# Two 128-partition loads per chunk, weight sums on VectorE, M on two queues, and an early half of chunk 0 in a cross-network kernel

## The chip, the cores and the metric

The kernel runs on one core of one Trainium2 chip. The metric is the device time in microseconds (us) of one execution, as a median of several; lower is better. The profile gives the span from the first to the last instruction of one execution.

## The reference

```python
def _cin_forward(x, Ws, bs, fc_w, fc_b):          # x: (1024, 64, 16) float32
    x0 = h = x; xs = []
    for i in range(3):
        z = einsum('bfe,bge->bfge', x0, h)         # all products of features
        y = einsum('oc,bce->boe', Ws[i], z.reshape(B, -1, 16)) + bs[i]   # 128 channels
        if i != 2: x_i, h = y[:, :64], y[:, 64:]   # one half is output, one goes on
        else:      x_i = h = y
        xs.append(x_i)
    return sum(concat(xs, 1), axis=2) @ fc_w.T + fc_b      # (1024, 1)
```

Only one weighted sum of the last channels is wanted. So the channel sums of the weights, V0, V1 and V2 (64x64 each), can be formed first, and V2 folded into the second layer's weights as a tensor M. For each column (one sample, one of 16 positions) the kernel then needs h1, the upper half of layer one, and q, a quadratic form made with M plus V1 x; the result is the sum of (h1 + b) q + x (V0 x + c).

## The kernel before

1024 samples are cut into 32 chunks of 512 columns. For a chunk VectorE makes four tiles z of products of features (128 partitions x 2048), TensorE contracts them with 16 weight tiles, and a 17th tile zl (squares and x itself) closes the sum. The 128 output rows are h1 (64) and q (64). This is the loop:

```python
def products(c, j):
    z = zp.tile([128, NI, N], F32, tag="z", name="z")              # zp has bufs=3
    nc.vector.tensor_tensor(z, xas[c], xbs[c][:, j, :]...to_broadcast(...), ALU.mult)
    for i in range(NI):
        t = j * NI + i
        nc.tensor.matmul(accs[c], w_all[:, t, :], z[:, i, :], start=(t == 0), stop=False)
...
for c in range(NCH + 1):
    if c + 1 < NCH: load_chunk(c + 1)      # four 64-partition loads, and zl, xx
    if c < NCH: products(c, 0); products(c, 1)
    if c > 0:   combine(c - 1)             # q, uu; each second chunk y = V0 x and the sums
    if c < NCH: products(c, 2); products(c, 3); squares(c)
```

Ahead of it stands a setup, in which each step needs the one before:

```python
for k in range(32):                        # V2 on TensorE, a moving operand of one column
    nc.tensor.matmul(pv2[:, k:k+1], w2s[:, k, :], fc2, start=True, stop=True)
... v2t ...                                # M = V2 times layer two's upper weights
nc.tensor.matmul(pm, v2t[to], w1s[to, m*512:(m+1)*512], start=True, stop=True)
...
nc.scalar.dma_start(out=md[0:64, 0:64, :], in_=m_sb)       # M to DRAM, 5 writes
nc.scalar.dma_start(out=ms1[to]..., in_=skewed(...))       # and back, 11 skewed reads
... w_all[:, 0:NT, 64:128] = ms1 + ms2                     # the q half of the weights
# V0 and V1: 8 products with a two-column weight tile, rows spread by more transfers
```

## Time and profile before

| | before |
|---|---|
| median time | 554.61 us (552.36 to 554.63) |
| span of the profile | 555.0 us |
| chunk 0 starts on TensorE | 66.3 us |
| chunk 1 starts | 80.9 us |
| last contraction ends | 546.3 us |

Three kinds of lines are read below. A line of the chain that ended last has a start, a length and what the chain was in. A group of instructions has its busy time and the mean ns of one, then after the bar the idle time of the engine just before it and what ended that. A line of the windows has the stretch, its length, the busy time of TensorE, weight loads, VectorE, ScalarE and GpSimd (each with its number of instructions), the granted clock, the share of the 16 DMA engines, and GB/s.

PE is TensorE, PEld its weight loads, DVE VectorE, ACT ScalarE; L191 is line 191 of that run's kernel file. A row of 40 digits has the busy share (or, as PEclk, the granted clock) of each fortieth of the span, in tenths. A queue is the order in which one engine (SyncE or ScalarE) issues its transfers. A group of TensorE counts two instructions for each product in the code. The lines of the kernel before stand in the prediction.

### The profile page before, as it was taken

The page shows a single profiled execution, that of the slowest core. Times are in us where ns is not written, and L with a number is a line of the kernel's source. Part 1 is how long each engine was busy: PE and PEld are TensorE (multiplying, and loading weights), DVE is VectorE, ACT ScalarE, POOL GpSimd, SP SyncE. Part 2 cuts the span into 40 slices and gives each one's busy share as a digit, 9 for nine tenths or more (in the row PEclk, how much of TensorE's full clock was granted, in tenths as well). Part 3 has the DMA queues.
Part 4 walks back from the last instruction along what each step waited for, and adds up shares of the span by engine and source line. Part 5 has one row for each costly group of instructions (what it writes and reads, how often), then busy time and mean ns, then how long its engine had stood idle before and what let it go on. Part 6 is the DMA issues. An engine that isn't in the chain of part 4 may idle for free.

```text
span 555.0 us, 3402 instructions
## 1 busy us (share of the span) xinstructions
PE 515.9 (93%) x1240; PEld 231.9 (42%) x1240; DVE 352.0 (63%) x205; ACT 44.9 (8%) x81; POOL 5.3 (1%) x18
## 2 busy tenths in 40 slices
PE   5803799999999999999999999999999999999997
PEld 5600144444444444444444444444444444444442
DVE  0250076768677677768676867767776867686751
ACT  0100300000000000000000000000000000000001
POOL 3000000000000000000000000000000000000000
PEclk9967699999999999999999999999999999999999
DMA  8999998787777777877778777777787877874000
GB/s 254 185 283 210 205 208 170 144 163 146 156 153 159 150 152 162 180 161 161 160 147 165 146 154 154 154 150 154 161 180 161 165 155 151 162 152 77 0 1 0
DMA packets 33114, 85.33 MB, mean 154 GB/s; under 512 B 6405, under 2 KB 6949, under 8 KB 28710
## 3 DMA queue, kind: packets, MB, share of 16 engines
q1 hardware_dynamic: 29234, 81.84, 71.1%
q10 hardware_dynamic: 3608, 3.28, 2.8%
q8 instruction: 10, 0.16, 0.2%
q14 instruction: 6, 0.05, 0.0%
q0 software_dynamic: 256, 0.00, 0.0%
HBM read 82.89 MB, written 2.17 MB: 153 GB/s over the span
## 4 chain that ended last, share of the span: by engine, by line
PE 92%; DMA 6%; DVE 0%; ACT 0%; issue 0%; ACTq 0%; SPq 0%
PE acc L236 79%; PE acc L240 5%; DMA w<-in_wv 3%; PE pv L133 2%; PE y L254 2%; PE pv L197 2%; DMA ms<-md 1%; DMA fc<-in_fc_w 1%; DMA md<-m_sb 1%; PE pm L146 1%; PE po L281 0%; DVE acc L256 0%; DVE uu L255 0%; ACT res L289 0%; ACT q L249 0%
## 5 line engine op out<-in xcount | busy, mean ns | idle before, releaser
L236 PE MATMUL acc<-z,w_all 128*128 128x512 f32 x1024 | 447.2, 592 | 0.0
L231 DVE TENSOR_TENSOR z<-xa,xb 128x2048 f32<-128x2048 f32 x128 | 293.3, 2292 | 135.9 <-PE acc L236 134.6
L236 PEld LDWEIGHTS acc<-z,w_all 128*128 128x128 f32 x1024 | 194.5, 190 | 244.5 <-issue 244.4
L249 ACT COPY q<-acc 64x512 f32<-64x512 f32 x32 | 18.6, 582 | 443.8 <-PE acc L240 443.8
L197 PE MATMUL pv<-w,fc 128*2 128x512 f32 x16 | 11.5, 887 | 27.9 <-DMA w<-in_wv 14.9
L240 PE MATMUL acc<-zl,w_all 128*128 128x512 f32 x64 | 32.7, 592 | 0.0
L250 DVE SCALAR_TENSOR_TENSOR uu<-acc,bh,q 64x512 f32<-64x512 f32 x32 | 23.7, 740 | 10.0 <-ACT q L249 9.5
L239 ACT ACTIVATE zl<-xa 64x512 f32<-64x512 f32 x32 | 20.1, 628 | 3.6 <-DMA xa<-in_x 3.6
L133 PE MATMUL pv<-fc,w2s 128*128 128x1 f32 x64 | 13.8, 352 | 6.6 <-DMA fc<-in_fc_w 6.6
L256 DVE TENSOR_REDUCE acc<-uu 128x64 f32<-128x1024 f32 x16 | 19.5, 1220 | 0.5
L240 PEld LDWEIGHTS acc<-zl,w_all 128*128 128x128 f32 x64 | 12.2, 190 | 15.3 <-issue 15.3
L197 PEld LDWEIGHTS pv<-w,fc 128*2 128x2 f32 x16 | 1.6, 108 | 37.6 <-issue 21.5
L133 PEld LDWEIGHTS pv<-fc,w2s 128*128 128x128 f32 x64 | 13.7, 332 | 6.6 <-DMA fc<-in_fc_w 6.6
L254 PE MATMUL y<-xx,bd 128*128 128x512 f32 x32 | 16.3, 592 | 0.0
L136 DVE COPY v2t<-pv 64x32 f32<-64x32 f32 x2 | 0.4, 184 | 20.4 <-PE pv L133 20.4
L255 DVE SCALAR_TENSOR_TENSOR uu<-y,cx,xx 128x512 f32<-128x512 f32 x16 | 11.9, 745 | 0.0
L188 DVE TENSOR_TENSOR w_all<-ms,ms 128x1024 f32<-128x1024 f32 x1 | 1.2, 1224 | 13.2 <-DMA ms<-md 13.2
L254 PEld LDWEIGHTS y<-xx,bd 128*128 128x128 f32 x32 | 6.1, 190 | 7.7 <-issue 7.7
L199 ACT COPY vrow<-pv 2x512 f32<-2x512 f32 x8 | 4.2, 570 | 33.3 <-DMA ms<-md 32.2
L184 DVE MEMSET ms<- 64x64 f32 x1 | 0.1, 112 | 9.7 <-DMA ms<-md 9.7
L146 PE MATMUL pm<-w1s,v2t 64*64 64x512 f32 x16 | 5.6, 809 | 0.5 <-DVE v2t L137 0.5
L152 DVE COPY m_sb<-pm 64x512 f32<-64x512 f32 x4 | 2.7, 683 | 3.2 <-PE pm L146 3.2
(33 smaller groups left out, 21.0 us busy)
## 6 DMA issues: line engine op xcount, KB each, us to landing
xa<-in_x SPq DMA_DIRECT2D x64, 512.0 KB, 5.8
xb<-in_x SPq DMA_DIRECT2D x64, 512.0 KB, 7.1
zl<-in_x SPq DMA_DIRECT2D x32, 128.0 KB, 4.2
xx<-in_x SPq DMA_DIRECT2D x32, 128.0 KB, 4.1
w2s<-in_wv SPq DMA_DIRECT2D x4, 512.0 KB, 7.8
w<-in_wv SPq DMA_DIRECT2D x4, 512.0 KB, 11.9
w1s<-in_w1h SPq DMA_DIRECT2D x1, 1024.0 KB, 13.4
md<-m_sb ACTq DMA_DIRECT2D x2, 512.0 KB, 7.1
```

Of the source, the lines that this page charges most:

```text
L133: nc.tensor.matmul(pv2[:, k : k + 1], w2s[:, k, :], fc2, start=True, stop=True)
L146: nc.tensor.matmul(pm, v2t[to], w1s[to, m * 512 : (m + 1) * 512], start=True, stop=True)
L197: nc.tensor.matmul(pv, fc01, w01[:, m * 512 : (m + 1) * 512], start=True, stop=True)
L231: nc.vector.tensor_tensor(z, xas[c], xbs[c][:, j, :].unsqueeze(1).to_broadcast([128, NI, N]), ALU.mult)
L236: nc.tensor.matmul(accs[c], w_all[:, t, :], z[:, i, :], start=(t == 0), stop=False)
L239: nc.scalar.activation(zls[c][0:64], xas[c][0:64, 0, :], AF.Square)
L240: nc.tensor.matmul(accs[c], w_all[:, NT, :], zls[c], start=False, stop=True)
L249: nc.scalar.copy(q, accs[c][64:128])
L250: nc.vector.scalar_tensor_tensor(uu[to, 0, :], accs[c][0:64], bh1, q, ALU.add, ALU.mult)
L254: nc.tensor.matmul(y, bd, xxs[c // 2], start=True, stop=True)
L255: nc.vector.scalar_tensor_tensor(uu[:, 1, :], y, cx, xxs[c // 2], ALU.add, ALU.mult)
L256: nc.vector.tensor_reduce(acc[:, :, c // 2, :], uu.rearrange("p k (b e) -> p k b e", e=E), AX.X, ALU.add)
```

## The change

Its intent is to shorten the setup and to keep VectorE well ahead of TensorE. Each chunk comes in two 128-partition loads. V2, V1 and V0 are made by a multiply and a reduction on VectorE. M is written and read on two queues, and the reads stand ahead of the V1 weights and of chunk 1. The h1 half of chunk 0 is contracted while M is under way: 64 output rows leave room for two column halves of the array, each taking 256 of the chunk's columns. The program order is fixed by hand, with three products ahead of the evictions; V0 is made inside chunk 2.

```diff
+    ctx.enter_context(tc.manual_schedule())
-    zp = ctx.enter_context(tc.tile_pool(name="zp", bufs=3))
+    zp = ctx.enter_context(tc.tile_pool(name="zp", bufs=7))
...
     def load_chunk(c):
-        for half in range(2):                      # 64 partitions each
-            nc.sync.dma_start(out=xa[to], in_=rows(c, 0, [[1, NI]]))
-            nc.sync.dma_start(out=xb[to], in_=rows(c, 16 * half + 4, [[4, NJ]]))
-        ... zl and xx loaded too
+        nc.sync.dma_start(out=xa, in_=...)         # 128 partitions, 8 KB rows
+        nc.sync.dma_start(out=xb, in_=xrb[c])      # zl and xx copied by ScalarE
...
+    def weigh(w, fc, out):
+        nc.vector.tensor_tensor(w, w, fc...to_broadcast(...), ALU.mult)
+        nc.vector.tensor_reduce(out, w, AX.X, ALU.add)
-    for k in range(32):
-        nc.tensor.matmul(pv2[:, k : k + 1], w2s[:, k, :], fc2, start=True, stop=True)
+    for k in range(4):
+        weigh(w2s[k // 2][:, cols], fcr[:, 128:256], v2h[:, 8 * k : 8 * k + 8])
...
+    nc.scalar.dma_start(out=md[0:64, 0:32, :], in_=m_lo)
+    nc.sync.dma_start(out=md[0:64, 32:64, :], in_=m_hi)
+    ... three more on sync, two more on scalar
...
+    def side_by_side(p, part, tiles):
+        for t in tiles:
+            for n in range(2):
+                nc.tensor.matmul(p[halves[n]], w_all[:, t, cols],
+                    z[:, n * H2 : (n + 1) * H2], start=(t == 0), stop=(t == NT))
+    side_by_side(ph, 0, range(NT + 1))             # h1 of chunk 0, before M is back
+    ... M read on two queues, then w1x and chunk 1 loaded
+    side_by_side(pq, 1, range(NT))                 # q of chunk 0
...
-    for c in range(NCH + 1):
+    for c in range(1, NCH + 1):
+        if c > 2 and c % 2 == 0: v0x(c // 2 - 1)   # y, ahead of the products
+            for j in range(NJ - 1): products(c, j)
+        ... factors(c - 1)                         # q, uu
+        if c == 2: ... weigh(w0x, ...); v0x(0)     # V0 made here, y after 3 products
+        if c % 2 == 0: sums(c // 2 - 1)
+            products(c, NJ - 1); last_tile(c); contract_last(c)
```

## The prediction

> **What bounds the kernel now.** I read four views. First the page: TensorE is the busiest engine, but the slices show two phases.
>
> ```profile
> span 555.0 us, 3402 instructions
> PE   5803799999999999999999999999999999999997
> PEclk9967699999999999999999999999999999999999
> L236 PE MATMUL acc<-z,w_all 128*128 128x512 f32 x1024 | 447.2, 592 | 0.0
> L231 DVE TENSOR_TENSOR z<-xa,xb 128x2048 f32<-128x2048 f32 x128 | 293.3, 2292 | 135.9 <-PE acc L236 134.6
> ```
>
> The first five slices (about 66 us) have holes and a lower granted clock; after them TensorE is at 9 to the end. L236 never idles (last column 0.0), and VectorE's L231 waits 134.6 us for TensorE: in the main loop TensorE is the bound and VectorE has slack. Second, the chain that ended last, start and length:
>
> ```profile
> 0.76 5.75 DMA fc<-in_fc_w
> 6.55 13.83 PE pv L133 x64
> ...
> 24.52 4.45 DMA md<-m_sb
> ...
> 29.36 11.91 DMA w<-in_wv
> 41.41 3.50 PE pv L197 x4
> 44.92 6.70 DMA w<-in_wv
> ...
> 52.26 6.73 DMA ms<-md
> ...
> 59.61 6.33 PE pv L197 x8
> ...
> 66.32 13.93 PE acc L236 x32
> 80.25 0.86 PE acc L240 x2
> 81.11 13.73 PE acc L236 x32
> ```
>
> The loop begins at 66.3; before it lies a serial setup: V2 on TensorE, M, M to DRAM and back (ms), V0 and V1 on TensorE. Third, the windows view (stretch, length, busy of PE, PEld, DVE, ACT, POOL, clock, DMA share, GB/s):
>
> ```profile
> 6.00:12.00 6.00, 5.45 (x26) 5.45 (x26) 0.00 (x0) 0.00 (x0) 0.33 (x3) 1.00 1.08 397
> 14.00:26.00 12.00, 11.52 (x46) 8.58 (x46) 2.59 (x7) 2.12 (x4) 0.00 (x0) 1.00 1.03 200
> 38.60:63.00 24.40, 8.59 (x13) 1.25 (x14) 1.45 (x3) 3.10 (x6) 0.00 (x0) 0.64 1.03 219
> 66.30:546.30 480.00, 480.00 (x1120) 212.62 (x1120) 336.38 (x186) 35.22 (x65) 0.00 (x0) 1.00 0.72 146
> ```
>
> The queues are full at 397 GB/s while 128-partition weights load and at 200 while the 64-partition halves of chunk 0 load. The loop is 480 us of unbroken TensorE. Fourth, the timeline of the end: the last contraction ends at 546.3, the span 8.7 us later (q, uu, reduction, po, store).
>
> **The Trainium skill.** "DMA: Bandwidth & Descriptors", Rules for kernel authors, advises one 128-partition transfer in place of two to disjoint halves; the 397 against 200 GB/s agree. "VectorE: DVE Perf Modes", the perf-mode tier table, has fp32 tensor_tensor and tensor_reduce at one element per cycle, 2293 ns for 2048; the trace has 2292 for L231 and 1220 for a reduction of 1024. "TensorE: Matmul & The Clock Gate", Part 1, says that idle of a few us halves the clock for the next 3.4 us or so; the trace grants 0.64 in the gappy stretch. "TensorEngine Tiling (Array Packing)", Tiling Modes, lets two 128x64 column tiles work independently; no run here shows column tiles. The row halves of L146 do overlap: 16 instructions took 5.6 us including 0.8 us for evictions and a cold start.
>
> **Part by part.** (1) *Main loop.* A logical 512-column product is two instructions, 0.858 us (16 in 13.73). A chunk is 17 of them, 14.59 us; 31 chunks and 15 V0 products are 452.4 + 12.9 = 465.3 us, unchanged, since TensorE is already unbroken. Fixed order, seven z buffers and three products of lead therefore buy nothing in the steady loop. The larger x transfers (2 MB instead of 2.25 MB a chunk) are hidden at a DMA share of 0.72 as well. The new ScalarE copies (three of about 0.6 us a chunk) sit on an engine with 2 us of work per 14.6.
>
> (2) *V2 on VectorE.* Removed: 13.8 us of TensorE. Added: four pairs of multiply and reduce over 1024, 4 x (1.22 + 1.22) = 9.8 us, beginning when the first weights and the broadcast row land, about 6.7 (the old row landed at 6.5). With four 0.2 us copies v2t is ready at 17.4 instead of 20.8. The M products then start cold: two pieces at 1.7 us, two at 0.86, plus an eviction of 0.7: M is in SBUF at 23.6, where the last old eviction ended at 27.2.
>
> (3) *M through DRAM.* Old: writes issued from 24.5, reads from 38.6 to 63.0, 24.4 us, on one queue, sharing the transfers with V weights and chunk loads. New: two queues, and the reads stand ahead of the V1 weights and chunk 1. Write: 2.1 MB, 1.6 us to start, between 5 us (397 GB/s) and 10 us (200), 2 us to land: I take 34. Reads: five issues of 0.63 us per queue and some 6 us of transfer, then queueing: SyncE's waits show an issue waiting for an older, unrelated load (8.3 us for zl behind xa), so I expect the third read on ScalarE's queue to wait for a first one. I take 44.7 for the last landing, and w_all's second half at 46 (1.22 us), against 64.2.
>
> (4) *Chunk 0 split.* h1 (17 tiles) runs on TensorE in the shadow of (3), z of chunk 0 ending at about 34 on VectorE. After 46 only the other half of the columns remains: 34 products of 256 columns. If column halves overlap, 7.3 us (half of 14.6) up to 9 if weight loads show; plus 1.7 us because the clock has fallen during the wait: start of chunk 1 at about 55.5. If they do not overlap, 14.6 + 1.7: 62.5. V1 (2.29 + 2.29 + 0.4 on VectorE) ends at about 51, beside this, if its 1 MB has landed by 46.
>
> (5) *V0 and order.* In chunk 2 the fixed order puts y after the third product on TensorE, and on VectorE uu, the reduction and the fourth z after y. When TensorE has finished y, VectorE needs 0.75 + 1.22 + 2.29 + 0.2 = 4.5 us more: one stall of 4.5 us, perhaps 0.9 of cold clock after it. From chunk 4 on y stands ahead of the chunk's products; after the eviction of chunk c-1, VectorE needs 0.7 + 0.75 + 2 + 2.29 = 5.8 us for the fourth z, wanted at 11.2. No stall.
>
> Sum: start of chunk 1 + 465.3 + 5.4 + 8.7. With 55.5: 534.9. With 62.5: 541.9. In the old kernel the same sum is 66.3 + 14.6 + 465.3 + 8.7 = 554.9, against 555.0 seen. So the gain is about 25 us of chunk 0 and setup less 5 us given back in chunk 2.
>
> **Rivals.** *A: column halves run one after the other.* For: no column tiles in this trace. Against: the row halves overlap. Weight 0.35; 542. *B: M's way through DRAM stays long.* The old reads took 8 to 10 us to land beside other transfers, and V1 weights and two chunks follow right behind on SyncE's queue; then w_all comes at 50 to 52 and the total is about 540 (547 with A). *C: M quick and overlapped, no clock loss:* writes at 397 GB/s and 3 us less in reads give w_all at 41, total 528 to 530. *D: the loop stops being unbroken*, VectorE or ScalarE becoming the bound through the fixed order: VectorE's work is 336 us of 480, so only a wrong order in every chunk would do it; 0.04, and then 560 or more is possible. *E: the gain lies in the loop* (the lead removing VectorE's waits): L236's idle of 0.0 speaks against it; those 134.6 us are waits of the engine with slack.
>
> **Range.** Mixing 0.65 x 535 and 0.35 x 542 with a few us of M's path either way gives a centre near 536; C pulls down. I say 535, 527 to 544. Faster by over 2% means below 543.5: only A with B, or D, miss it: 0.87. Within 2%: 0.11. Slower: 0.02.
>
> **What would show it.** Chain: the loop starts (first chunk-1 product) at 52 to 63; L133 and L197 gone. Windows: TensorE unbroken after it but for one gap of 4 to 5 us some 26 us later, waiting for z. V2 reduction ends at 17, last M read lands at 42 to 48. The second pass over chunk 0 lasts 9 to 11 us if halves overlap, 15 to 17 if not. Spacing of full products stays 0.429 us per instruction, the tail 8.7. I am wrong if TensorE shows regular gaps in every chunk, if chunk 1 starts after 65, or if the chunk-2 stall is absent (then 5 us better).

## The result, and the profile after

| | before | after |
|---|---|---|
| median time | 554.62 us (4 runs) | 538.23 us (537.95 to 539.22, 4 runs) |
| span of the profile | 555.0 | 536.1 |
| chunk 1 starts | 80.9 | 55.9 |

The ratio is 0.9717, with a 95% interval of 0.969 to 0.9745: the mean time of the changed kernel's runs over that of the other's runs of the same rounds, so not quite the ratio of the medians. Executions over 1.5% slower than the fastest of the same kernel are left out of the means. The change is 2.8% faster.

The page of the changed kernel has these lines for those shown of before:

```profile
span 536.1 us, 3189 instructions
PE   0465996999999999999999999999999999999997
PEclk9987998999999999999999999999999999999999
L191 PE MATMUL acc<-z,w_all 128*128 128x512 f32 x992 | 432.8, 594 | 4.7 <-DVE z L182 4.7
L182 DVE TENSOR_TENSOR z<-xa,xb 128x2048 f32<-128x2048 f32 x128 | 284.5, 2281 | 1.6 <-DMA xb<-in_xrb 1.5
L214 DVE SCALAR_TENSOR_TENSOR uu<-acc,bh,q 64x512 f32<-64x512 f32 x31 | 23.1, 744 | 138.0 <-ACT q L213 138.0
L153 PE MATMUL pm<-w1s,v2t 64*64 64x512 f32 x16 | 5.9, 863 | 17.3 <-DVE v2t L143 17.3
L239 PE MATMUL pq<-z,w_all 128*64 128x256 f32 x64 | 8.4, 429 | 9.1 <-DVE w_all L280 9.1
```

The setup now takes four slices of 13.4 us instead of five of 13.9. VectorE's products no longer wait for TensorE (134.6 us before, nothing now); but VectorE's slack has only moved, for its uu now waits 138.0 us for q, the copy of a finished sum. TensorE, which never waited inside the loop before, now waits 4.7 us for a z (0.4 before chunk 1, 4.3 in chunk 2). The chain that ended last tells the setup and where those 4.7 us lie:

```profile
0.75 6.40 DMA fcr<-in_fc_w
...
17.26 5.93 PE pm L153 x16
...
25.17 8.63 DMA md<-m_sb
...
33.86 2.33 DMA md<-m_sb
...
37.81 4.62 DMA ms<-md
...
42.85 10.59 DMA xb<-in_xrb
...
53.56 2.30 DVE z L182
55.91 14.00 PE acc L191 x32
...
81.07 0.87 PE y L222 x2
...
81.96 0.76 DVE uu L226
...
83.89 2.29 DVE z L182
...
86.22 5.40 PE acc L191 x8
```

V2 is done at 17.2, M is written until 36.2 and its two large tiles are read until 44.6, and chunk 1 starts at 55.9. The chain reaches chunk 1 through its load (xb lands at 53.4) and its first z, which ends at 55.9; the second pass over chunk 0 had ended at 55.5. In chunk 2, y ends at 81.9, then uu, the reduction and the fourth z follow one another on VectorE, and TensorE resumes at 86.2. Eight instructions then take 5.40 us instead of 3.43. Four windows, of the second pass over chunk 0, the stall, the time after it, and the loop:

```profile
46.10:55.50 9.40, 9.38 (x76) 5.55 (x76) 6.87 (x5) 0.41 (x2) 0.00 (x0) 0.86 1.02 426
82.00:86.00 4.00, 0.00 (x0) 0.00 (x0) 3.97 (x3) 0.00 (x0) 0.00 (x0) 1.00 0.01 2
86.00:90.00 4.00, 3.78 (x5) 1.65 (x6) 4.00 (x3) 0.00 (x0) 0.00 (x0) 0.57 0.71 262
100.00:527.00 427.00, 427.00 (x996) 189.05 (x995) 291.01 (x167) 65.69 (x112) 0.00 (x0) 1.00 0.32 126
```

The granted clock is 0.57 in the 4 us after the stall, which is where the 2 us went. In the loop TensorE is again busy for every one of 427 us; the share of the DMA engines is 0.32, less than half of the 0.72 before.

The balance: chunk 1 starts 25.0 us earlier, chunk 2 gives back 4.3 us of stall and 2.0 of clock, and 25.0 less 6.3 is 18.7, against 18.9 in the spans. By stages of the two traces, the 25.0 are:

| stage | before | after | gain |
|---|---|---|---|
| M's last eviction ends | 27.2 | 23.9 | 3.3 |
| from there to w_all's second half | 37.0 | 22.1 | 14.9 |
| from there to chunk 0 (the second pass) | 2.0 | 0.1 | 1.9 |
| from there to chunk 1 | 14.7 | 9.8 | 4.9 |

The largest share is M's way through DRAM. The third line is the last of V0 and V1 on TensorE, which in the kernel before ended 2 us after the weights were ready.

### The profile page after: what moved, and what is told of

Read it like the earlier page. It is cut to its first block, busy times and chain, and to the rows that moved or that the text cites. A ratio compares the mean times of both kernels' runs of the same rounds, so it can differ in the third digit from the quotient of the medians.

```text
span 536.1 us, 3189 instructions
## 1 busy us (share of the span) xinstructions
PE 496.6 (93%) x1262; PEld 222.0 (41%) x1262; DVE 362.1 (68%) x222; ACT 79.1 (15%) x135; POOL 5.7 (1%) x18
## 3 DMA queue, kind: packets, MB, share of 16 engines
q1 hardware_dynamic: 12058, 74.82, 36.2%
## 4 chain that ended last, share of the span: by engine, by line
PE 89%; DMA 6%; DVE 3%; issue 0%; ACTq 0%; SPq 0%; ACT 0%; DVEq 0%
PE acc L191 80%; PE acc L205 5%; PE y L222 2%; DMA md<-m_sb 2%; DMA xb<-in_xrb 2%; DMA fcr<-in_fc_w 1%; PE pm L153 1%; DVE v2h L133 1%; DVE w L132 1%; DMA ms<-md 1%; DVE z L182 1%; PE po L354 0%; DVE uu L226 0%; DVE acc L227 0%; ACTq L271 0%
## 5 line engine op out<-in xcount | busy, mean ns | idle before, releaser
L191 PE MATMUL acc<-z,w_all 128*128 128x512 f32 x992 | 432.8, 594 | 4.7 <-DVE z L182 4.7
L191 PEld LDWEIGHTS acc<-z,w_all 128*128 128x128 f32 x992 | 188.9, 191 | 243.4 <-issue 230.0
L182 DVE TENSOR_TENSOR z<-xa,xb 128x2048 f32<-128x2048 f32 x128 | 284.5, 2281 | 1.6 <-DMA xb<-in_xrb 1.5
L214 DVE SCALAR_TENSOR_TENSOR uu<-acc,bh,q 64x512 f32<-64x512 f32 x31 | 23.1, 744 | 138.0 <-ACT q L213 138.0
L205 PE MATMUL acc<-zl,w_all 128*128 128x512 f32 x62 | 31.7, 592 | 0.0
L153 PE MATMUL pm<-w1s,v2t 64*64 64x512 f32 x16 | 5.9, 863 | 17.3 <-DVE v2t L143 17.3
L197 ACT COPY zl<-xa 64x512 f32<-64x512 f32 x32 | 19.7, 615 | 0.4
L201 ACT COPY xx<-xa 64x512 f32<-64x512 f32 x32 | 19.6, 614 | 0.4
L239 PE MATMUL pq<-z,w_all 128*64 128x256 f32 x64 | 8.4, 429 | 9.1 <-DVE w_all L280 9.1
L239 PE MATMUL ph<-z,w_all 128*64 128x256 f32 x64 | 8.8, 444 | 4.5 <-DVE w_all L170 4.5
L153 PEld LDWEIGHTS pm<-w1s,v2t 64*64 64x64 f32 x16 | 2.9, 196 | 19.4 <-DVE v2t L143 17.3
L239 PEld LDWEIGHTS pq<-z,w_all 128*64 128x64 f32 x64 | 5.0, 157 | 12.5 <-DVE w_all L280 9.6
L132 DVE TENSOR_TENSOR w<-w,fcr 128x1024 f32<-128x1024 f32 x4 | 4.9, 1217 | 7.2 <-DMA fcr<-in_fc_w 7.2
L239 PEld LDWEIGHTS ph<-z,w_all 128*64 128x64 f32 x64 | 5.3, 160 | 8.5 <-DVE w_all L170 5.4
```

The source lines that it names most:

```text
L153: nc.tensor.matmul(pm[to], v2t[to], w1s[to, cols], start=True, stop=True)
L182: nc.vector.tensor_tensor(z, xas[c], xbs[c][:, j, :].unsqueeze(1).to_broadcast([128, NI, N]), ALU.mult)
L197: nc.scalar.copy(zl[64:128], xas[c][64:128, 0, :])
L201: nc.scalar.copy(xxs[c // 2][to], xas[c][to, 0, :])
L205: nc.tensor.matmul(accs[c], w_all[:, NT, :], zls[c], start=False, stop=True)
L214: nc.vector.scalar_tensor_tensor(uus[c // 2][to, 0, :], accs[c][0:64], bh1[0:64], q, ALU.add, ALU.mult)
```

## The experiments

Twelve runs in three groups, each group on one chip with its own runs of the kernel before; all results were correct. A ratio is to the kernel before. The changed kernel itself has 0.9717 in its first measurement and 0.9751 as a control in the third group, so that differences of up to 0.0035 (2 us) between groups mean nothing by themselves; below that I go by the stages in the profiles. Part of that noise is the clock: in the ten profiles that keep the stall of chunk 2, the eight instructions after it took 5.17 to 6.53 us. "Chunk 1" is when chunk 1 starts on TensorE.

| run | median us | ratio | span | chunk 1 |
|---|---|---|---|---|
| changed kernel | 538.23 | 0.9717 | 536.1 | 55.9 |
| z before the sums | 532.64 | 0.9621 | 529.7 | 55.5 |
| short lead | 539.88 | 0.9750 | 536.2 | 56.0 |
| chunk 0 whole | 546.83 | 0.9881 | 544.8 | 64.1 |
| M on ScalarE's queue | 551.50 | 0.9962 | 549.9 | 69.2 |
| V2 on TensorE | 545.65 | 0.9862 | 545.2 | 64.0 |
| chunks in halves | 546.56 | 0.9883 | 544.7 | 62.2 |
| M's corner | 538.11 | 0.9725 | 536.5 | 55.8 |
| clock kept up | 536.10 | 0.9693 | 533.8 | 53.1 |
| control | 539.72 | 0.9751 | 537.4 | 57.3 |
| M on SyncE's queue | 541.13 | 0.9769 | 538.5 | 57.4 |
| combined | 528.59 | 0.9554 | 526.5 | 52.3 |
| chunk 1 early | 529.02 | 0.9554 | 526.2 | 52.1 |

**1. The fourth z of chunk 2 before the sums.**

```diff
+        if c == 2:
+            products(c, NJ - 1)
         if c % 2 == 0:
             sums(c // 2 - 1)
         if c < NCH:
-            products(c, NJ - 1)
+            if c != 2: products(c, NJ - 1)
```

> Edit: in chunk 2 alone the fourth product is made and contracted before the sums of pair 0, so VectorE no longer waits for y before it makes that z. Theory (the fixed order of chunk 2 costs one stall of 4.3 us and 2.0 us of halved clock after it): the gap at 82 us disappears and the span falls from 536.1 by 6.3 us to 529.8; the time from 538.2 to about 532. Rival (VectorE is simply out of time there, because the V0 reduction adds 4.6 us in one piece): z is still late and at most 2 to 3 us come back.

The span is 529.7, to 0.1 us what the theory asked for (0.4 of the 6.4 us lie before chunk 1, in this execution's earlier start). VectorE's timeline in chunk 2 of this run (start, length, and in brackets the wait before it):

```profile
77.26 2.29 DVE L182 TENSOR_TENSOR z<-xa,xb 128x2048 f32<-128x2048 f32 x1
81.53 0.75 DVE L226 SCALAR_TENSOR_TENSOR uu<-y,cx,xx 128x512 f32<-128x512 f32 x1 [1.98 <-PE y L222]
82.32 1.22 DVE L227 TENSOR_REDUCE acc<-uu 128x64 f32<-128x1024 f32 x1
```

The z is made in the time in which VectorE formerly waited 4.3 us for y. VectorE had the time all along, so the rival (4.6 us of V0 reduction are too much) falls: the order was at fault.

**2. A short lead in the loop.** From chunk 3 on, two products ahead and three z buffers, as before:

```diff
+    zq = ctx.enter_context(tc.tile_pool(name="zq", bufs=3))
-        z = zp.tile(...)
+        z = (zq if c > 2 else zp).tile(...)
-            for j in range(NJ - 1): products(c, j)
+            for j in range(NJ - 1 if c < 3 else NJ - 2): products(c, j)
...
+            if c > 2: products(c, NJ - 2)
             products(c, NJ - 1)
```

> Edit: from chunk 3 on, two products ahead instead of three before the factors, and three z buffers of their own instead of sharing seven, as in the kernel before. Theory (TensorE was already unbroken in the loop, the lead buys nothing there): no change, within 0.5 us of 538.2, and no idle time of TensorE after 100 us. Rival (the lead and the seven buffers are part of the gain): gaps in every chunk or every second one, 10 us or more in all.

The span is 536.2, and TensorE has no wait between 95 us and the last reduction. The median of 539.88 lies 1.65 us above the first median of the changed kernel and 0.16 above the control's; so the times exclude a loss of 10 us but not one of 1 us, and the trace excludes that too. The lead and the seven buffers buy nothing in the loop.

**3. Chunk 0 like every other chunk.** `side_by_side` is dropped; the 16 tiles of 128 rows and zl follow `w_all`.

```diff
-    side_by_side(ph, 0, range(NT + 1))
...
-    side_by_side(pq, 1, range(NT))
+    new_acc(0)
+    for t in range(NT):
+        nc.tensor.matmul(accs[0], w_all[:, t, :], zs[t // NI][:, t % NI, :], ...)
...
-    side_by_side(pq, 1, [NT])
+    contract_last(0)
... q and uu of chunk 0 as in every other chunk
```

> Edit: chunk 0 is contracted like every other chunk, 17 products of all 128 columns after the second half of w_all, nothing in the shadow of the M transfer. Theory (the column halves overlap, so the early h1 saves half of chunk 0's TensorE time): the second pass of 9.4 us becomes 14.6 us and 1.7 us of halved clock, chunk 1 starts at about 62.5 instead of 55.9, and the time is 6.6 us longer (about 545). Rival (column halves do not overlap, each narrow product costs like a full one): no change within 1 us.

The span is 8.7 us longer. The 16 tiles stand in the chain as

```profile
46.03 16.67 PE acc L280 x32
```

where the split has 9.4 in all; zl and the small products add 1.4, which my 62.5 had left out, and the clock after the stall of chunk 2 another 0.8. The column halves overlap and the early h1 is worth some 8 us.

**4. All of M on ScalarE's queue.**

```diff
-    nc.sync.dma_start(out=md[...], ...)            # four writes
+    nc.scalar.dma_start(out=md[...], ...)
-        queue = (nc.sync, nc.scalar)[half]
+        queue = nc.scalar
```

> Edit: all writes and reads of M on ScalarE's queue, the order otherwise kept. Theory (two queues save issue time only, some 3 us of the ten reads at 0.63 us each): the last read lands 2 to 4 us later than 44.6, the time is 2 to 4 us longer. Rival (the transfers themselves run faster from two queues): writes take 5 us longer and reads 3 us, 8 us or more in all.

13.8 us of span were lost, as the rival said, but not for its reason. Two pieces of the chain of this run:

```profile
31.69 6.90 DMA md<-m_sb
...
38.61 4.48 DMA md<-m_sb
...
43.24 6.61 DMA ms<-md
```

The last two, small writes took 6.9 and 4.5 us; in the changed kernel the last took 2.33. SyncE, with no M transfer of its own to wait for, issued the V1 weights at 16.8 us, chunk 1 at 19.2 and 21.8, and V0 and chunk 2 at 31.6 to 33.0, beside M's writes and reads. The experiment had changed two things at once: the number of queues and what the loads wait for. Run 9 parts them.

**5. V2 on TensorE.** The 32 products and the old layout of the weights:

```diff
+    nc.scalar.dma_start(out=fc2, in_=fc_w[0, 128:256].unsqueeze(1))   # after fcr
...
-        weigh(w2s[k // 2][:, cols], fcr[:, 128:256], v2h[:, 8 * k : 8 * k + 8])
+    for k in range(32):
+        nc.tensor.matmul(v2h[:, k : k + 1], w2s[k // 16][:, at : at + 128], fc2, ...)
```

> Edit: V2 made on TensorE as in the kernel before (32 products with a one-column moving operand, 13.8 us), the weights in their old layout; all else as after. Theory (V2 stands alone at the head of the path that ends with M, and all of its length counts): v2t is ready at about 20.8 instead of 17.3 and the whole kernel is 3.5 us longer. Rival (M's way is bounded by the weight load of W1 or by the write queue, so V2 has slack): less than 1 us.

More than expected: 9.1 us of span, and 6 to 8 us by the ratios (its runs spread from 543.16 to 547.15, and the profiled one is the slowest). The group and the next one:

```profile
L141 PE MATMUL pv<-fc,w 128*128 128x1 f32 x64 | 13.8, 352 | 8.6 <-DMA fc<-in_fc_w 8.6
L157 PE MATMUL pm<-w1s,v2t 64*64 64x512 f32 x16 | 6.6, 951 | 0.5 <-DVE v2t L147 0.5
```

M's products begin at 22.8 instead of 17.3: 13.8 us of products instead of 9.7 on VectorE, and a start at 8.6 instead of 7.2, because the column of 4-byte pieces landed at 8.4. This is an effect of the edit, which issues it second; in the kernel before it was issued first and landed at 6.5. Another 2.5 us came before chunk 1, of which 0.7 in M's products and 1.3 in the second pass and the start after it, and 1.1 us after the stall of chunk 2 (6.53 us instead of 5.40), where V2 has no part. So the delay of M's products is 5.6 us and that of V2's own length 4.1, where the theory had 3.5; the rest of the 9.1 is not shown to be V2's.

**6. Chunks in 64-partition halves.**

```diff
-        nc.sync.dma_start(out=xa, in_=...[[N, 128], [1, NI * N]])
-        nc.sync.dma_start(out=xb, in_=xrb[c])
+        for n, to in enumerate(halves):
+            nc.sync.dma_start(out=xa[to], in_=...[[N, F], [1, NI * N]])
+            nc.sync.dma_start(out=xb[to], in_=xrb[c][to])
```

> Edit: every chunk is loaded in four 64-partition transfers (same 8 KB rows, same bytes). Theory (the large transfers are hidden in the loop and matter only in the head): the loop stays unbroken; the loads of chunk 1 behind the M reads take about 5 us longer, so that chunk 1 starts 3 to 7 us later, and the time is 3 to 7 us longer. Rival 1 (loads are hidden everywhere): no change. Rival 2 (loads bind in the loop): gaps in many chunks and 15 us or more.

Chunk 1 starts at 62.2, 6.3 us later, since its xb lands at 59.7 instead of 53.4; its first 32 instructions take 16.53 us instead of 14.00, at a granted clock of 0.84. That is 8.8 us, against 8.6 in the span. In the loop nothing happens, although the DMA engines have twice the work for the same bytes:

```profile
100.00:500.00 400.00, 400.00 (x933) 177.08 (x932) 283.19 (x162) 63.26 (x108) 0.00 (x0) 1.00 0.64 140
```

TensorE is busy for all 400 us, at a DMA share of 0.64 instead of 0.32. The large transfers pay in the setup and are hidden in the loop.

**7. The overlapping corner of M's small writes.**

```diff
-    nc.sync.dma_start(out=md[64:68, 64:96, :], in_=m_lo[0:4])
+    nc.sync.dma_start(out=md[64:68, 68:96, :], in_=m_lo[0:4, 4:32, :])
```

> Edit: the last small write of M leaves out the four columns that the write before it has already written, so the two no longer overlap. Theory (the last write waited 6.8 us for the other because both write the same corner, and the reads wait for it): the last write lands at about 34.3 instead of 36.2, everything after it comes 1.9 us earlier, 1.9 us in all. Rival (the reads would wait anyway for the large writes or for free places in the queue): under 0.5 us.

A miss. The last write is issued 6 us earlier and no longer waits, but the writes as a whole still take 11.4 us from M's last eviction to the first read (12.3 before), 0.9 us less and not 1.9, since one of the larger ones lands only at 35.5. M itself came 0.5 us later in this execution. The ratio, 0.9725, cannot be told from the changed kernel's.

**8. The clock kept up.** Unused products, 18 ahead of M and 19 ahead of the second pass; they read the broadcast row and nothing reads their sum:

```diff
+    def keep_warm(n, name):
+        p = ps.tile([128, 256], F32, tag="y", name=name, bufs=1)
+        for _ in range(n):
+            nc.tensor.matmul(p, fcr[:, 0:128], fcr, start=True, stop=True)
+    keep_warm(18, "warm_a")
...
+    keep_warm(19, "warm_b")
```

> Edit: unused products keep TensorE busy ahead of the M products and ahead of the second pass over chunk 0 (their result is never read). Theory (M's products lose about 1.9 us to the halved clock, the second pass about 1.3 us, but the first z of chunk 1 is ready only 0.4 us before the end of that pass, so the second loss is hidden): M is ready 1.9 us earlier, chunk 1 starts 2 to 2.5 us earlier, and the time is 2 to 2.5 us shorter. Rival 1 (both losses count in full): 3.2 us. Rival 2 (the clock does not matter in the head): nothing, or longer because the unused products are in the way.

The span is 2.3 us shorter, within the theory's 2 to 2.5. By the ratios it is 1.3 us against the first measurement, 3.2 against the control. M's products and the second pass, as groups:

```profile
L245 PE MATMUL pq<-z,w_all 128*64 128x256 f32 x64 | 7.1, 381 | 0.7 <-DVE w_all L286 0.7
L159 PE MATMUL pm<-w1s,v2t 64*64 64x512 f32 x16 | 3.7, 595 | 0.0
```

3.7 us instead of 5.9, and 7.1 instead of 8.4; the first of these began 0.8 us late, since the unused products overshot. Chunk 1 starts at 53.1, right after its z, which ends only then. The windows view does not show the slow clock of M's products in the changed kernel: it has 1.00 from 19 to 24 us. In the trace the first record of the clock stands at 21.5 us, and the view counts the time ahead of it as full; there the instructions of M's products go over from one each 0.43 us to one each 0.21.

**9. All of M on SyncE's queue**, so that the V1 weights and chunk 1 stay behind it, with the changed kernel on the same chip as control (run 12, unaltered).

```diff
-    nc.scalar.dma_start(out=md[...], ...)          # three writes
+    nc.sync.dma_start(out=md[...], ...)
-        queue = (nc.sync, nc.scalar)[half]
+        queue = nc.sync
```

> Edit: all writes and reads of M on SyncE's queue, so that the V1 weights and the chunk loads still stand behind them (with everything on ScalarE's queue they did not, and the loads ran beside M's small writes). Theory (what that run lost was the loads running ahead; a second queue in itself saves only issue time): the loss shrinks from 13.3 us to 2 to 4 us, w_all's second half at 48 to 50. Rival (one queue is slow in itself for M): again 8 us or more.

> The changed kernel itself, unaltered, as a control on the same chip as the three runs beside it. Expected: 538.2 us and a ratio of 0.972 to the kernel before, the span of the profile 536 to 537.5; the start of chunk 1 within 0.5 us of 55.9. What it differs by is the noise against which small effects of the other runs are judged.

It is 1.4 us longer than the control by the medians, 1.1 by the spans, and chunk 1 starts 0.1 us later; the last read of M's tiles lands at 44.9. Of the 1.1 us, 1.0 is the clock after the stall of chunk 2 (6.41 us instead of 5.40). Before it, M's way from the issue of its first write to w_all took 22.5 us here and 22.6 in the control; the second pass was 1.3 us slower, at a granted clock of 0.74 instead of 0.84, and M had come 0.9 us earlier. The rival falls, and even the theory expected too much: no gain of a second queue is seen in M's way. The 13 us of run 4 came from the loads that ran ahead: the sixth write, issued at 31.7 there and at 31.3 here, landed at 38.6 and at 33.9, and the reads took 14.2 us there and 8.7 here. (Runs 4 and 9 also differ in the engine that issues, ScalarE or SyncE; that is not parted.) The control came out 1.5 us above the first measurement, 1.4 of it before chunk 1: M's products took 6.71 us in it instead of 5.93, with no change in the program.

**10. The parts together:** runs 1 and 7, and run 8 with 16 and 18 unused products.

> Edit: the fourth z of chunk 2 ahead of the sums, the two small writes of M no longer overlapping, and TensorE kept busy by unused products (16 and 18) ahead of M's products and of the second pass. Theory (the effects lie one after the other on the path, so they add): 6.3 us from chunk 2, 2.3 from the clock of M's products, 0.5 to 0.9 from the small write: span 526.5 to 527.5, time about 529, ratio 0.955 to 0.958. Rival (they overlap): 530 or more in the span.

528.59 us and 0.9554, on the chip of the control: 11.1 us under it, and 4.5% under the kernel before. It begins the main loop at 52.3 with no stall after. In the chain, its setup leads through the unused products:

```profile
36.28 7.97 PE warm_b L150 x36
44.25 7.06 PE pq L245 x64
```

The weights for the second pass were ready at 43.2, so eighteen unused products were some two too many. The expected sum was right: span 526.5 to 527.5.

**11. Chunk 1 loaded before M, its first z made early.**

```diff
     nc.sync.dma_start(out=w0u, in_=w0b)
+    load_chunk(1)
...
     side_by_side(ph, 0, range(NT + 1))
+    made = {(1, j): product(1, j) for j in range(2)}
...
+    keep_warm(19, "warm_b")                        # 18 in the combined kernel
```

> Edit: as the combined kernel, and chunk 1 is loaded before M is written (the queues stand at 76 GB/s from 19 to 24 us), and its first two z are made while VectorE waits for M to come back, ahead of w_all's second half and V1. Theory (the first z of chunk 1, made after V1, ends 0.6 us after the second pass would and hides the clock's second gain): chunk 1 starts right after the second pass, 1.5 to 2 us earlier than in the combined kernel, span about 525. Rival (loading chunk 1 then slows the writes of M by as much as it gains): no better than the combined kernel, w_all 2 us later.

529.02 us, the same 0.9554: a miss. In the combined kernel the second pass ended at 52.3, as late as the first z of chunk 1 (52.2), so an earlier z alone gains nothing. In run 11 the last read of M's tiles landed at 42.4 instead of 41.8 and the second pass, from 44.0, ended at 52.1.

## Why the prediction was right

- **The loop is untouched and the gain lies in the setup:** right. TensorE was unbroken in the loop before and after, and run 2 takes the lead away without loss. Rivals D and E fall.
- **V2:** v2t was to be ready at 17.4 and M in SBUF at 23.6 (the terms named add up to 23.2); the trace has 17.2 and 23.9. Run 5 has the direction: V2 on TensorE takes 4.1 us longer and nothing on the way to chunk 1 takes that up. More of its loss is not V2's length, as said there.
- **M through DRAM:** I took 34 for the writes, 44.7 for the last read and 46 for the weights; measured were 36.2, 44.6 and 46.0. The writes term was 2.2 us too small and the reads term as much too large, so that 44.7 is right by luck. Run 7 takes the wait between the two small writes away and finds 0.9 of the 2.2 us there; the rest is open. On each queue it was the fifth read, not the third, that waited until the first had landed (at 40.1 and 41.2). Rival B (reads held up by the loads) did not occur, because the loads stand behind them; run 4 shows that it is real, by 13 us.
- **Chunk 0 split:** the second pass was to last 9 to 11 us if the halves overlap; it lasted 9.4, and run 3 confirms it with 8 us. Rival A falls. Rival C did not come about. That chunk 1 then started at 55.9, where I had 55.5, is partly luck: the working followed the second pass alone (ended at 55.5), and the chain goes through chunk 1's load and z, which it had not named as a limit.
- **Chunk 2:** one stall of 4.5 us and 0.9 of clock; measured 4.3 and 2.0. Run 1 removes it by order alone. The clock term was 1.1 us too small, in this execution; in the ten profiles with the stall it was 1.7 to 3.1.
- **The distance of 3.2 us to the median** thus has two parts. The span came out at 536.1 instead of 534.9, of which the clock in chunk 2 explains 1.1. The other 1.9 us is no step of the working: I set the span equal to the time, because the profiled run of the kernel before, at 556.8, happened to lie 2 us above that kernel's median. A time of 534.9 would need a span of 533. The centre was also drawn low: 0.65 x 535 and 0.35 x 542 give 537.5, not "near 536".
- **The large loads** I called hidden. In the loop they are, but run 6 shows 6.3 us in the start of chunk 1 that the working had not named; in it the old chunk loads simply vanished into the old setup's length. A smaller slip: two of ScalarE's three operations on a chunk's tiles are new, not three; its busy time per chunk went from 1.1 to 2.2 us of 14.6, and TensorE did not wait for it.

The effects of runs 3, 5 and 6 are not shares of the 25.0 us: each was taken out alone, and they share waits. The table of stages says where the 25.0 us were gained. Which edit earned the 14.9 us of M's way (order of the loads, fewer and larger loads, two queues) is open: no run changes one of these in the kernel before, and runs 4 and 9, in the changed kernel, speak for the order and against the second queue. The fixed order as such was not taken away in any run either.

## What to carry to other kernels

Before a reorder is credited with a gain, look whether the engine that sets the pace ever waits. VectorE's waits, 134.6 us ahead of its products, only went to another instruction (138.0 us) when they were removed there, and the price of a fixed order can sit in one odd iteration, as chunk 2 shows with 6.3 us. In a serial setup count each step from the landing that starts it, ask what the clock is when its products begin, and hold later loads back behind a transfer that everything waits for. When an experiment moves a transfer to another queue, check what the instructions left on the old queue then no longer wait for.

## What the Trainium skill lacked or had wrong

- "DMA: Bandwidth & Descriptors", Issuing engines are not separate DMA queues, says that a second queue saves only issue time. Run 9 agrees: from the first write of M to w_all, one queue took 22.5 us and two 22.6. It lacks the side effect: a queue that waits also holds back what stands behind it, and with that gone 13.8 us of span were lost (run 4).
- "TensorEngine Tiling (Array Packing)", Tiling Modes, has no measured time for two 128x64 tiles in float32, and no other page has. Here 64 instructions of 256 columns took 7.1 us when the clock was kept up (run 8), where 32 full ones of 512 columns take 13.73.
- "TensorE: Matmul & The Clock Gate", Part 1, speaks of the clock after activity. It does not say whether products with a one-column moving operand count as such: after 13.8 us of them, M's products took 6.6 us (run 5), no faster than after idle time (5.6 to 6.7 in the other runs of the changed kernel without unused products), and 3.7 after ordinary products (run 8).
